# Staging the padded projection weights in an exponentials' buffer, with the query part compacted later

## The chip, the cores and the metric

The kernel runs on one core of one Trainium2 chip. A core has a matrix engine (TensorE, PE in the profile; its weight loads are shown as PEld), a vector engine (VectorE, DVE), an engine for activations and scaled copies (ScalarE, ACT), a general engine (GpSimd, POOL) and a queue engine (SyncE, SP). Each runs its own instructions in order and waits for the others on semaphores. ScalarE, GpSimd and SyncE also issue DMA transfers. SBUF is the on-chip memory, PSUM the memory that TensorE writes to.

The metric is the device time of one execution in microseconds (us), as the median of several runs.

## The reference

Input x has 4 batches of 1024 tokens of 256 features. The function is one transformer block, each half with a norm before it and a norm of what it adds:

```
x = x + layernorm(attention(layernorm(x), Wqkv, Wout))
x = x + layernorm(ffn(layernorm(x), w1, w2, h1, h2, w3 and scales))

attention: q, k, v = x @ Wqkv.T in 16 heads of 16
           softmax(q k^T / 4) v, then @ Wout.T
ffn:       h = silu(x w1^T s1) * (x w2^T s2)
           h = gelu(h h1^T t1);  h = gelu(h h2^T t2);  h w3^T s3
```

The weights of the feed-forward part hold only -1, 0 and 1. All is float32.

## The kernel before, in words

The attention goes over 4 batches, in each over 4 groups of 4 heads (`HPG`), in each over two halves of 512 queries, and in each over 8 chunks of 128 keys. For a chunk and two heads a score tile `s` of 128 x 1024 is made by two matmuls (line 471), ScalarE writes its exponentials `e` (line 472), and four matmuls add `e` times the values into `acc` (line 479). The exponentials lie in a ring of four buffers, `ring` (line 227), each for two score tiles. The first ring buffer is also zeroed at the start (`zeros`, line 228), and matmuls of these zeros into the tile `idle` (line 979) keep TensorE at work while the first input arrives. The feed-forward part follows after all four batches.

Scores are exact to about float32 though they are made with a shorter format: the projections are split into a rounded part (`hi`, line 330, by ScalarE) and the rest (`lo`, line 331, by VectorE). DMAs copy rows of both into stacked operands `sk` and `sq` (lines 410 to 423, issued in line 419), so that one matmul sums the products of the parts. For the first batch there are 64 such copies: 16 for each of k and q in each of the two halves of the tokens. Their issue is dealt out over three engines in turn (line 975): in every 8 copies ScalarE issues one, GpSimd four and SyncE three.

What comes before the first score tile, for batch 0, is the prologue, in this order. SyncE issues the load of the first half of x, the key part of the projection weights `wqk`, the second half of x, and the query part of `wqk` (lines 153 and 189 to 193). `wqk` is padded in memory: each head has 32 columns (`SLOT`), of which 16 (`DH`) hold weights. It lands in a staging tile, `slotted`, and ScalarE copies the 16 columns of each head into the dense tile `wqk_sb` (line 191), first the key part (`w` = 1), then the query part (`w` = 0). The staging tile is in a pool of its own, `load`, at the right side of SBUF, which is closed after these copies. The pool `work` is opened at the right side after it (line 239).

VectorE takes the mean and variance of x's rows (lines 96 and 97), GpSimd the root (`rstd`, line 106), and VectorE writes the normalised rows into `xn`, a tile of the pool `work` (line 297, recorded at line 114). TensorE transposes `xn` into `pt` (line 307), ScalarE copies that to `xT` (line 308, recorded at line 268), and TensorE projects: k first, then q (`project`, lines 322 to 333; the matmuls are recorded at line 265, their output is `p`). After each projection the stack copies are issued. All that is done for the first half of the tokens and then for the second. Then come the first values `v[0]` (`pv`, copied to `cv`), and the score tiles begin. GpSimd places the values into `vaug` (line 449), which `acc` needs.

All of it is emitted in the order of the program (`manual_schedule`, line 152): each engine executes what it is given in the order in which the code calls it. The loop that orders the prologue is in lines 983 to 992. In the attention's main loop, side work (projections of further batches, values, endings) is put between the tiles by a planner, `Side`, which counts slots and does not look at the hardware; the change does not touch it.

Of the kernel before, what the change touches and what calls it, by code (L numbers as in the profile page):

```python
# [9 lines left out]
F32 = mybir.dt.float32  # L10
# [8 lines left out]
P = 128  # L19
HEADS = 16  # L20
DH = 16
SLOT = 32
# [4 lines left out]
RING = 8  # L27
# [10 lines left out]
NQ = 512  # L38
# [4 lines left out]
@with_exitstack  # L43
def tile_attention_ffn_block(ctx: ExitStack, tc: tile.TileContext, x, wqk, wv, wo, w1, w1s, w2, w2s, h1, h1s, h2, h2s, w3, w3s, out):

    nc = tc.nc
    B, S, D = x.shape
    bad = ctx.enter_context(tc.tile_pool(name="flag", bufs=1)).tile([1, 1], I32, name="bad")
    tile_fast(tc, x, wqk, wv, wo, w1, w1s, w2, w2s, h1, h1s, h2, h2s, w3, w3s, out, bad)
    failed = nc.values_load(bad[0:1, 0:1], min_val=0, max_val=1 << 24)
    with tc.If(failed > 0):
        tile_general(tc, x, wqk, wv, wo, w1, w1s, w2, w2s, h1, h1s, h2, h2s, w3, w3s, out)  # L70
# [47 lines left out]
def tile_fast(ctx: ExitStack, tc: tile.TileContext, x, wqk, wv, wo, w1, w1s, w2, w2s, h1, h1s, h2, h2s, w3, w3s, out, bad):  # L118
    nc = tc.nc
    B, S, D = x.shape  # L120
    HID = w1.shape[1]
    DC = D // P
# [17 lines left out]
    def pieces(h, view):  # L140

        t, n = NH + (TPQ - 1) * h, TPQ * h
        return (slice(n, n + 1), view[:, h : h + 1, :]), (slice(n + 1, n + TPQ), view[:, t : t + TPQ - 1, :])

    def load_x(b, halves=range(NH)):
        view = x[b].rearrange("(t p) d -> p t d", p=P)
        for h in halves:
            for at, tokens in pieces(h, view):
                nc.sync.dma_start(out=xs[b][:, at, :], in_=tokens)
# [31 lines left out]
    with ExitStack() as actx, ExitStack() as rctx:  # L181
        aw = actx.enter_context(tc.tile_pool(name="aw", bufs=1, side="right"))

        wqk_sb = aw.tile([P, DC, 2, HEADS, DH], F32, name="wqk_sb")
        wv_sb = aw.tile([P, DC, D], F32, name="wv_sb")
        wo_sb = aw.tile([P, DC, D], F32, name="wo_sb")
        with tc.tile_pool(name="load", bufs=1, side="right") as load:
            slotted = load.tile([P, DC, 2, HEADS, SLOT], F32, name="slotted")
            for w in (1, 0):
                nc.sync.dma_start(out=slotted[:, :, w], in_=wqk.rearrange("(c p) (k h s) -> p c k h s", p=P, k=2, s=SLOT)[:, :, w])  # L190
                nc.scalar.copy(wqk_sb[:, :, w], slotted[:, :, w, :, 0:DH])
                if w:
                    load_x(0, [1])
        nc.scalar.dma_start(out=wv_sb, in_=wv.rearrange("(c p) d -> p c d", p=P))

        def load_rest():
# [23 lines left out]
        for i in range(2):  # L220
# [1 line left out]
            nc.gpsimd.memset(t, 0.0)  # L222
            nc.gpsimd.memset(t[:, :, :, DH : DH + 1], 1.0)
            vaug.append(t)

        rp = rctx.enter_context(tc.tile_pool(name="ring", bufs=1))
        ring = [rp.tile([P, 2, 2, NQ], F32, name=f"e{i}") for i in range(RING // 2)]
        zeros = ring[0][:, 0, 0]
        nc.vector.memset(zeros, 0.0)

        on = [aw.tile([P, TPQ, D], F32, name=f"on{h}") for h in range(NH)]

# [177 lines left out]
        def copies(g, w, c0=0, c1=S):  # L410

            m, i = g // GPT, g % 2

            def copy(u, j, n):
                def run(queue):
                    k = "hi" if (j // 2 == 0 if w == 0 else j % 2 == 0) else "lo"
                    r = (g % GPT) * HPG * DH + (2 * u + n) * DH
                    o = n * ROWS + j * DH
                    queue.dma_start(out=stacks[w, i, u][o : o + DH, c0:c1].bitcast(F32), in_=cq[w, m, k][r : r + DH, c0:c1].bitcast(F32))

                return run

            return [copy(u, j, n) for u in range(2) for j in range(PARTS) for n in range(2)]
# [33 lines left out]
        stacked, slotted, outstanding = [None] * 2, [None] * 2, []  # L457
# [201 lines left out]
        side = Side()  # L659
# [323 lines left out]
        for h in range(NH):  # L983
            for step in xt[h][TPQ // 2 :]:
                step.run()
            for w, step in zip((1, 0), qk[0][h]):
                step.run()
                for i, copy in enumerate(copies(0, w, h * NQ, (h + 1) * NQ)):
                    copy(queues[i % len(queues)])
                if w and h + 1 < NH:  # L990
                    for step in normalise[h + 1]:
                        step.run()
# [18 lines left out]
        while weighed < len(tiles):  # L1011
            n = end = made
# [3 lines left out]
            if made == len(tiles):  # L1016
                n = made
# [4 lines left out]
            if n - weighed >= 4 and made - weighed + TURN - 2 <= RING and tiles[weighed][3] != NT - 2 and side.next_is_heavy():  # L1022
                n = weighed + 2
            while weighed + 2 <= n:
                b, g, h, c, _ = tiles[weighed]
# [258 lines left out]
```

## Time and profile before

| what | value |
|---|---|
| time before, median of 3 runs | 1292.86 us (1292.04 to 1293.14) |
| span of the profiled execution | 1291.6 us |
| its own time outside that span | not given apart; the median of the runs is 1.26 us above the span |
| TensorE busy | 1244.4 us, 96% of the span |
| VectorE busy | 729.1 us, 56% |
| ScalarE busy | 699.2 us, 54% |
| GpSimd busy | 120.2 us, 9% |
| DMA traffic | 107.03 MB, mean 83 GB/s |
| first start of `acc` (line 479) | 34.34 us after the span's start |

The page of the profile describes one execution. It gives each engine's busy time, the span cut into 40 slices with the busy share in tenths, and the chain of work that ended last. Other answers of the trace list who waited for whom, the instructions in order of time (start, length, engine, line, operation, tile written and tiles read, and in brackets the idle time before it and what ended that), and for chosen stretches the busy time of each engine with the clock that TensorE was granted as a share of full speed.

### The profile page before, as it was taken

What the parts mean: (1) busy time and instruction counts of PE and PEld (TensorE: products, weight loads), DVE (VectorE), ACT (ScalarE), POOL (GpSimd) and SP (SyncE); (2) the same over time, 40 slices, a digit from 0 to 9 for tenths busy, and PEclk for the clock granted to TensorE, in tenths of its full rate; (3) what the DMA queues carried; (4) which work ended last, traced back from release to release, by engine and by line L of the source; (5) the groups of instructions that cost most, each with busy time, mean ns of one, the idle gap of its engine ahead of it and who ended that gap; (6) DMA issues with size and microseconds to landing.
All of it is one profiled execution on the core that took longest, in us unless ns stands there. A gap on an engine that the chain in (4) does not pass through costs nothing.

```text
span 1291.6 us, 21098 instructions
## 1 busy us (share of the span) xinstructions
PE 1244.4 (96%) x8104; PEld 770.0 (60%) x8104; DVE 729.1 (56%) x1625; ACT 699.2 (54%) x855; POOL 120.2 (9%) x166
## 2 busy tenths in 40 slices
PE   7999999999999999998999999999999999999995
PEld 3333334333333334333788888888888888888885
DVE  3466557765677556755643725637456374463533
ACT  3788788888889888998421413214132141331410
POOL 6211012111121110000000000000000000000000
PEclk8999899999999999999999999999999999999998
DMA  4676644665574654462320000201102011020000
GB/s 130 159 188 161 146 121 119 145 162 122 117 178 117 154 117 100 99 163 85 134 92 1 25 1 1 74 17 41 49 1 66 25 42 49 1 66 9 17 1 20
DMA packets 65679, 107.03 MB, mean 83 GB/s; under 512 B 12960, under 2 KB 39200, under 8 KB 65568
## 3 DMA queue, kind: packets, MB, share of 16 engines
q1 hardware_dynamic: 57680, 80.93, 25.4%
q0 software_dynamic: 7360, 24.12, 6.0%
q8 instruction: 66, 1.08, 0.4%
q10 hardware_dynamic: 528, 0.52, 0.2%
q14 instruction: 45, 0.37, 0.1%
HBM read 48.38 MB, written 23.59 MB: 56 GB/s over the span
## 4 chain that ended last, share of the span: by engine, by line
PE 76%; DVE 10%; ACT 8%; issue 2%; DMA 2%; SPq 1%; ACTq 0%; POOL 0%; POOLq 0%; DVEq 0%
PE ph L814 36%; PE acc L479 13%; PE s L471 8%; ACT e L472 6%; PE pz L867 4%; PE p L265 4%; PE pg L814 3%; PE py L265 2%; PE pv L265 2%; DVE sg L830 2%; DVE top L488 2%; DVE ha_lo L819 1%; DVE st L96 1%; PE po L518 1%; ACT sg L828 1%
## 5 line engine op out<-in xcount | busy, mean ns | idle before, releaser
L472 ACT ACTIVATE e<-s 128x1024 f32<-128x1024 f32 x512 | 482.6, 1035 | 59.4 <-PE s L471 49.7
L479 PE MATMUL acc<-e,vaug 128*32 128x512 f32 x2048 | 256.8, 604 | 1.4 <-POOL vaug L449 1.3
L850 ACT ACTIVATE a<-ph,h_scale 128x512 f32<-128x512 f32 x128 | 81.0, 685 | 301.4 <-PE ph L814 301.4
L471 PE MATMUL s<-sq,sk 64*128 64x512 f32 x1024 | 186.0, 443 | 18.2 <-ACT e L472 13.4
L814 PE MATMUL ph<-hb_hi,h 128*128 128x512 f32 x512 | 199.5, 390 | 0.0
L814 PE MATMUL ph<-hb_lo,h 128*128 128x512 f32 x512 | 199.4, 389 | 0.0
L471 PEld LDWEIGHTS s<-sq,sk 64*128 64x128 f32 x1024 | 86.1, 185 | 139.0 <-ACT e L472 114.6
L488 DVE TENSOR_TENSOR top<-top,e 128x512 f32<-128x512 f32 x192 | 134.8, 702 | 16.0 <-ACT e L472 10.8
L106 POOL TENSOR_TENSOR rstd<-ve,minus_half 128x4 f32<-128x4 f32 (+1 forms) x33 | 38.3, 1162 | 834.9 <-DVE ve L104 834.9
L479 PEld LDWEIGHTS acc<-e,vaug 128*32 128x32 f32 x2048 | 49.3, 109 | 107.1 <-issue 102.8
L814 PEld LDWEIGHTS ph<-hb_lo,h 128*128 128x128 f32 x512 | 96.1, 188 | 20.1
L814 PEld LDWEIGHTS ph<-hb_hi,h 128*128 128x128 f32 x512 | 96.1, 188 | 20.2
L851 DVE CAST ha_hi<-a 128x512 fp32r<-128x512 f32 x64 | 27.1, 423 | 142.7 <-ACT a L850 142.7
L814 PE MATMUL ph<-ha_hi,sq 128*128 128x512 f32 x256 | 101.8, 398 | 0.4
L814 PE MATMUL ph<-ha_lo,sq 128*128 128x512 f32 x256 | 99.8, 390 | 0.0
L814 PE MATMUL ph<-ha_lo,sk 128*128 128x512 f32 x256 | 99.7, 390 | 0.0
L814 PE MATMUL ph<-ha_hi,sk 128*128 128x512 f32 x256 | 99.7, 389 | 0.0
L828 ACT ACTIVATE sg<-pg,w_scale 128x512 f32<-128x512 f32 x64 | 43.3, 688 | 56.0 <-DVE ha_lo L819 45.6
L830 DVE SCALAR_TENSOR_TENSOR sg<-pg,w_scale,sg 128x512 f32<-128x512 f32 x64 | 47.1, 745 | 46.3 <-ACT sg L828 46.1
L851 DVE CAST hb_hi<-a 128x512 fp32r<-128x512 f32 x64 | 27.0, 422 | 71.5 <-ACT a L850 71.5
L265 PE MATMUL p<-xT,wqk_sb 128*32 128x512 f32 x512 | 62.3, 608 | 2.9 <-DVE on L496 1.7
L814 PEld LDWEIGHTS ph<-ha_hi,sq 128*128 128x128 f32 x256 | 48.1, 188 | 13.1 <-DVE sg L830 3.4
(165 smaller groups left out, 1640.7 us busy)
## 6 DMA issues: line engine op xcount, KB each, us to landing
w<-in_h_dram POOLq DMA_DIRECT2D x16, 512.0 KB, 5.6
h_r<-wr POOLq DMA_DIRECT2D x16, 512.0 KB, 3.8
x<-in_h_dram SPq DMA_DIRECT2D x32, 256.0 KB, 2.7
top_d<-top SPq DMA_DIRECT2D x30, 256.0 KB, 2.3
folded<-top_d SPq DMA_DIRECT2D x30, 256.0 KB, 3.3
sk<-ck1hi SPq DMA_DIRECT2D x64, 64.0 KB, 2.7
sk<-ck1lo SPq DMA_DIRECT2D x64, 64.0 KB, 2.9
sq<-cq1hi SPq DMA_DIRECT2D x64, 64.0 KB, 2.6
```

Of the source, the lines that this page charges most:

```text
L106: nc.gpsimd.tensor_tensor(rstd[:, :n], ve[:, :n], self.minus_half[:, :n], ALU.pow)
L265: nc.tensor.matmul(o[j : j + SLOT, :], w[:, j : j + SLOT], i, **flags)
L471: nc.tensor.matmul(s[:, a, :], stacks[1, g % 2, u][r, c * P : (c + 1) * P], stacks[0, g % 2, u][r, h * NQ : (h + 1) * NQ], start=True, sto ...
L472: nc.scalar.activation(pair(k)[:, u], s, AF.Exp)
L479: nc.tensor.matmul(acc[SLOT * i : SLOT * (i + 1), :], vaug[g % 2][:, c, i, :], pair(k)[:, i // 2, i % 2, :], start=c == 0, stop=c == NT - 1)
L488: nc.vector.tensor_max(top, top if c > 1 else pair(k - 2)[:, :, :, 0:P], pair(k)[:, :, :, 0:P])
L814: nc.tensor.matmul(p, homes[n][c][:, m * P : (m + 1) * P], half[:, c, :], start=c == 0 and k == 0, stop=c == len(homes[n]) - 1 and k == 1)
L828: nc.scalar.activation(sg, p[:, 0, :], AF.Silu, scale=scales["w1"][:, m : m + 1])
L830: nc.vector.scalar_tensor_tensor(sg, p[:, 1, :], scales["w2"][:, m : m + 1], sg, ALU.mult, ALU.mult)
L850: nc.scalar.activation(a, p[:, j, :], AF.Gelu, scale=scales[n][:, m : m + 1])
L851: nc.vector.tensor_copy(o[0][:, m, :], a)
L867: nc.tensor.matmul(p[t], half[:, c, t * P : (t + 1) * P], homes["w3"][c], start=c == 0 and k == 0, stop=c == HC - 1 and k == 1)
```

## The change

The staging tile and its pool are taken away. The ring of exponentials' buffers is allocated earlier, at the place where the staging pool was, with the zeroing of its first buffer. The padded weights are loaded into the last ring buffer, seen with the shape of the staging tile, by the same two DMAs in the same order. The two copies into `wqk_sb` become calls of `compact`: the one for the key part follows directly after the loads' issue; the one for the query part is called in the prologue's loop, for the first half of the tokens, between k's stack copies and q's projection. In ScalarE's order it so comes behind the copies of the first transposed x, k's rounded part and the two stack copies that ScalarE issues for k; the load of the values' weights, `wv`, is issued before it and no longer after it.

```diff
@@ -184,13 +184,20 @@
-        with tc.tile_pool(name="load", bufs=1, side="right") as load:
-            slotted = load.tile([P, DC, 2, HEADS, SLOT], F32, name="slotted")
-            for w in (1, 0):
-                nc.sync.dma_start(out=slotted[:, :, w], in_=wqk.rearrange("(c p) (k h s) -> p c k h s", p=P, k=2, s=SLOT)[:, :, w])
-                nc.scalar.copy(wqk_sb[:, :, w], slotted[:, :, w, :, 0:DH])
-                if w:
-                    load_x(0, [1])
+        rp = rctx.enter_context(tc.tile_pool(name="ring", bufs=1))
+        ring = [rp.tile([P, 2, 2, NQ], F32, name=f"e{i}") for i in range(RING // 2)]
+        zeros = ring[0][:, 0, 0]
+        nc.vector.memset(zeros, 0.0)
+        padded = ring[-1].rearrange("p a b n -> p (a b n)").rearrange("p (c k h s) -> p c k h s", c=DC, k=2, s=SLOT)
+
+        def compact(w):
+            nc.scalar.copy(wqk_sb[:, :, w], padded[:, :, w, :, 0:DH])
+
+        for w in (1, 0):
+            nc.sync.dma_start(out=padded[:, :, w], in_=wqk.rearrange("(c p) (k h s) -> p c k h s", p=P, k=2, s=SLOT)[:, :, w])
+            if w:
+                load_x(0, [1])
+        compact(1)
         nc.scalar.dma_start(out=wv_sb, in_=wv.rearrange("(c p) d -> p c d", p=P))
@@ -222,11 +229,6 @@
-
-        rp = rctx.enter_context(tc.tile_pool(name="ring", bufs=1))
-        ring = [rp.tile([P, 2, 2, NQ], F32, name=f"e{i}") for i in range(RING // 2)]
-        zeros = ring[0][:, 0, 0]
-        nc.vector.memset(zeros, 0.0)
@@ -984,6 +986,8 @@
             for w, step in zip((1, 0), qk[0][h]):
+                if (h, w) == (0, 0):
+                    compact(0)
                 step.run()
                 for i, copy in enumerate(copies(0, w, h * NQ, (h + 1) * NQ)):
```

## The prediction

> **What bounds the kernel now.** First the page: TensorE is busy 96% of the span and makes up 76% of the chain, so time is lost only where it waits. In its 40 slices the first alone shows 7.
>
> ```profile
> PE 1244.4 (96%) x8104; PEld 770.0 (60%) x8104; DVE 729.1 (56%) x1625; ACT 699.2 (54%) x855; POOL 120.2 (9%) x166
> ...
> PE   7999999999999999998999999999999999999995
> ```
>
> So I read the first 40 us: waits, then the chain, then the timeline. The waits (who for whom, total, times, longest) show VectorE held 3.9 us by ScalarE's copy of the weights, and TensorE by VectorE behind it:
>
> ```profile
> DVE xn L114 <- ACT wqk_sb L191: 3.9, 1, 3.9
> PE pt L307 <- DVE xn L114: 3.1, 1, 3.1
> ```
>
> Normalising reads no weights. The code explains the wait: `xn` is in a pool opened where the staging tile's pool was closed, on the same side, so it takes that memory over. The timeline shows when `xn` could have started: its last real input, `rstd`, ends at 6.38+1.03=7.41; it starts at 10.15.
>
> ```profile
> 6.38 1.03 POOL L106 TENSOR_TENSOR rstd<-ve,minus_half 128x4 f32<-128x4 f32 x1 [2.89 <-DVE ve L104]
> 9.44 0.62 ACT L191 COPY wqk_sb<-slotted 128x512 f32<-128x512 f32 x1 [2.67 <-DMA slotted<-in_wqk_dram]
> 10.15 1.38 DVE L114 TENSOR_SCALAR xn<-x,mv,rstd 128x256 f32<-128x256 f32 x4 [3.86 <-ACT wqk_sb L191]
> ```
>
> The chain (start, length, what) runs through that copy and k's projection, then through the issue of stack copies, whose last query copy releases the scores at 28.81:
>
> ```profile
> 3.17 6.25 DMA slotted<-in_wqk_dram
> 9.44 0.62 ACT wqk_sb L191
> ...
> 12.92 3.62 PE p L265 x16
> 16.56 0.61 ACT ck0hi L268
> ...
> 25.80 2.81 DMA sq<-cq0lo
> ...
> 33.89 0.40 POOL vaug L449
> 34.29 0.04 issue
> 34.34 1.06 PE acc L479 x8
> ```
>
> I measure all by the start of `acc` at 34.34: after it the engines release each other in a fixed order, and I pass a shift there 1:1 to the end.
>
> Last the windows cut at the clock's steps (PE busy, then, after the other engines, the granted clock). Full clock is lost after 1.38 and 1.93 us of work in 3.41 us, and kept after 2.00 (101.73):
>
> ```profile
> 6.16:9.57 3.41, 1.38 (x4) 0.31 (x2) 0.14 (x1) 0.74 (x2) 1.03 (x1) 1.00 0.69 252
> 9.57:12.98 3.41, 2.36 (x12) 1.61 (x16) 2.73 (x10) 1.12 (x3) 0.00 (x0) 0.50 0.30 77
> 12.98:16.40 3.41, 3.41 (x20) 0.79 (x22) 0.82 (x4) 0.57 (x1) 1.01 (x1) 0.50 0.00 0
> 26.64:30.05 3.41, 1.93 (x14) 1.13 (x18) 0.00 (x0) 2.13 (x3) 3.41 (x8) 1.00 0.61 138
> 30.05:33.46 3.41, 3.41 (x34) 1.59 (x24) 0.41 (x1) 1.43 (x2) 3.04 (x7) 0.50 0.57 119
> 101.73:105.14 3.41, 2.00 (x21) 0.89 (x15) 2.32 (x5) 1.37 (x2) 0.00 (x0) 1.00 0.19 58
> ```
>
> [...] steps at 9.57, 16.40, 30.05 and 33.46 lie on a grid of 3.41; four matmuls of k's projection take 0.85 us before 16.40 and 0.43 after. That the grid's phase differs between executions one profile can't show. [...] 2.30 us of transposes in 9.57 to 12.98 didn't raise the clock. [...]
>
> **The change part by part.** *Removed: the wait of `xn`.* It starts 0.05 after `rstd`, at 7.45: 2.70 earlier. The rest of the first half's chain, to k's rounded copy `ck0hi`, took 16.56-10.15=6.41 at half clock.
>
> *Clock.* The warming matmuls end at 7.53. Today the array idles until 10.62 and falls to half at 9.57. With transposes from 7.9 the window to 9.57 holds 1.38+1.65=3.0 us of work, so I expect full clock to stay. k's 16 records then take 4x0.43=1.71 for 3.41, the transposes before some 0.25 less: `ck0hi` starts at 7.45+6.41-1.95=11.9, which is 4.65 earlier.
>
> *Moved: the query copy, 0.62 us.* It comes after k's projection in program order, so on ScalarE behind `ck0hi` (0.60) and two DMA issues (17.18 to 18.42, 1.24). From `ck0hi`'s start: 0.60+0.03+1.24+0.04=1.91, copy 0.62, 0.07 to release: q's projection starts 2.60 later, where today it follows k's at once. At 1.71+0.24, `cq0hi` starts at 11.9+4.55=16.5; today at 16.56+1.91. So q is 2.64 later relative to k. Who waits? POOL and SP are issuing k's copies till 5.1 and 5.4 after `ck0hi` started (21.67 and 21.96 today); q's rounded part, 4.55+0.60+0.28=5.4, is 0.3 late for POOL, nothing for SP. Without that cover it would be 2.64.
>
> *What is late next.* TensorE takes q, then the second half's transposes: `cq0hi` to transposed x 1.85 (18.47 to 20.31), 0.65 to k, 1.99 to its `ck0hi`: 16.5+4.49=20.9, end 21.5, first POOL copy 21.8. POOL has been free since 21.0 and issues 16 copies at 0.476 until 29.4, against 33.09 today: 3.7 earlier. TensorE meanwhile ends the second half (8x0.43 from 19.8, no waits), the first values (1.73, done 25.1) and three score tiles to 25.8; the second values take 1.73 to 27.7 for 3.33 today, as the gap between 26.3 and 28.8 that cost the clock is gone. Their copy (0.74+0.14) is done before POOL, so `vaug` starts at 29.5 and `acc` at 29.95: **4.4 earlier in this grid**.
>
> *Other phases.* Today's half-clock stretch at 30.05 is chance. In a grid where the gap at 26.3 to 28.8 loses no window, the second values end 1.6 earlier and `vaug` waits for POOL's 33.09 instead: `acc` at 33.6, 0.7 earlier. I give that half the grids: -0.35. After the change, the array idles from 11.8 to 14.5; a window whose end falls between 13.9 and 16.2 goes to half within q, costing 1.7 where it ends ahead of 14.5 and the rest of q's time after it: (0.6x1.7+1.7x0.85)/3.41, -0.72 on average. k at half in a tenth of the grids: 0.1x1.95, -0.2. Sum 4.4-0.35-0.72-0.2=**3.1 us**.
>
> *Costs of nothing.* Weights land in the last ring buffer: same bytes, same two issues at the same places of SP's queue; its first exponential is tile 6, after 37 us, on the engine that read it. The zeroing of the first ring buffer keeps its place on VectorE. The `wv` load (256 KB, 1 issue) goes out at 6.8, no longer 9.45, into traffic of some 400 GB/s: others land up to 0.7 later. x's second half (8.13) is read from 8.9 to 10, the query weights (9.42) at 13.8; uncovered it would cost 0.7. The key copy stays at 6.16.
>
> Sum against the profiled execution: span 1291.6-3.1=1288.5. The median is 1292.86, 1.26 above that span (what lies around it, and spread); kept as it is: **1289.8 us**.
>
> **Rivals.** *A, likeliest: as above,* 2 to 4.6 us faster, 1288.2 to 1290.9.
>
> *B: k stays at half clock[...].* For it: 1.38 us of matmuls lost the clock[...]. Against: the window at 101.73 kept it with 2.00, of which 0.76 transposes. Then `ck0hi` starts near 13.4 to 13.9, q at 16.0 to 16.5, partly at half, `cq0hi` near 19.3, the second half's `ck0hi` at 23.8, POOL done at 32.3, `acc` at 32.8 to 33.5: 0.9 to 1.5 faster, 1291.7, inside the noise.
>
> *C, slower: the gap before q breaks the clock for the whole second half.* From `cq0hi` 20.15 (k and q at half), second k starts 22.65; the second projections, both pairs of values take 6.9 at full and 13.7 at half. At full `acc` comes at 32.8; all at half, 39.6: 5.3 late, 1298.1. It decides (2.6 late) from 4.1 of the 6.9 on. Against it: 12.98 to 16.40 shows that one full window restores the clock.
>
> *D: the wait stays,* because `xn` or the transposes hang on something else that lands at 9.4; then q's 2.64 less POOL's cover of 2.4 leaves 1293.1. The listed waits of `xn` name only the weights and `rstd`, so hardly.
>
> **How the numbers follow.** Below 0.2%, 2.6 us, a measurement of this kernel tells nothing from no change. A 0.68, of which 0.50 above 2.6 us; B 0.18, D 0.04, C 0.10 with other losses. Faster 0.50; same 0.18+0.18+0.04=0.40; slower 0.10. Unknown are the clock's phases (each half-clock window later, like 142.69 to 149.52, is worth up to 1.7), so the range goes beyond A: low 1287.0 (4.4 and one such window saved, near 6), high 1293.8 (B and D plus half a window); A's own is 1288.2 to 1290.9.
>
> **What would show it.** Right: `xn` at 7.4 to 7.6, k's 16 records within 2.0 us, the query copy at 13.8 behind two DMA issues with 2.7 us of idle TensorE around it, POOL's last stack copy near 29.4, `acc` near 30, `vaug` waiting on POOL rather than the values' copy. Wrong: granted clock 0.5 between 9.6 and 13, second values again at half, or a later stretch at half clock that eats the 4 us.

## The result and the profile after

The changed kernel takes 1288.69 us (median, 1287.05 to 1291.96), the kernel before beside it 1293.14: ratio 0.9969, 95% interval 0.9956 to 0.9981. Measured again later, beside other runs of before, it took 1290.17 against 1293.01: ratio 0.9982, 0.9974 to 0.9991. In microseconds the two intervals are 2.5 to 5.7 and 1.2 to 3.4 faster. Single runs of either kernel spread over some 5 us and more. The mean of all 28 runs of the changed kernel is 1290.1, of before 1293.1 to 1293.2 in each of the later sets: 3.0 us or 0.23% faster. The forecast was 1289.8, 3.1 faster, which lies inside both intervals.

The wait of `xn` is gone. In the timeline of the changed kernel it follows `rstd` at once (7.35), k's rounded part `ck0hi` starts at 11.79 and no longer at 16.56, and the copy of the query weights stands at 13.70, behind two issues of DMAs on ScalarE's queue (ACTq). Its weights had landed long before: in the kernel below that keeps both copies at the head, the same copy ran at 9.53.

```profile
6.28 1.03 POOL L106 TENSOR_TENSOR rstd<-ve,minus_half 128x4 f32<-128x4 f32 x1 [2.79 <-DVE ve L104]
7.35 1.38 DVE L114 TENSOR_SCALAR xn<-x,mv,rstd 128x256 f32<-128x256 f32 x4 [1.15 <-POOL rstd L106]
...
9.80 1.92 PE L267 MATMUL p<-xT,wqk_sb 128*32 128x512 f32 x16 [0.25 <-ACT xT L270]
...
11.79 0.60 ACT L270 ACTIVATE ck0hi<-p 128x512 fp32r<-128x512 f32 x1 [1.55 <-PE p L267]
12.42 1.24 ACTq L421 DMA_DIRECT2D sk<-ck0hi  x2
...
13.70 0.62 ACT L194 COPY wqk_sb<-e 128x512 f32<-128x512 f32 x1 [1.31 <-issue]
```

k's 16 records take 1.92 us to the last end, at full clock. In the chain, which counts to the next engine's start, they take 1.97, where the half-clock ones of before took 3.62. In place of the wait stands a new one, named in the list of waits for the first 40 us:

```profile
PE p L267 <- ACT wqk_sb L194: 2.6, 1, 2.6
```

In the windows cut at the steps of this execution's clock (PE busy, then, last but two, the granted clock) that gap leaves 0.77 us of work between 11.67 and 15.09; q, from 14.37 on, mostly ran at half:

```profile
8.26:11.67 3.41, 3.16 (x23) 1.10 (x23) 2.63 (x11) 1.09 (x2) 0.53 (x1) 1.00 0.25 86
11.67:15.09 3.41, 0.77 (x12) 0.29 (x12) 2.02 (x5) 1.22 (x2) 2.85 (x6) 1.00 0.22 48
15.09:18.50 3.41, 3.41 (x18) 1.43 (x11) 0.46 (x1) 0.60 (x1) 2.03 (x5) 0.50 0.52 106
18.50:21.91 3.41, 2.21 (x23) 0.77 (x25) 0.23 (x1) 1.09 (x2) 3.41 (x8) 1.00 0.51 106
```

At the end of the prologue, by the timeline, the values' copy is done at 29.32+0.69=30.01, but `vaug` starts when GpSimd has issued its last stack copies, at 30.90. `acc` starts at 31.36, before it was 34.34: 2.98 earlier.

```profile
29.32 0.69 DVE L273 TENSOR_SCALAR cv<-pv 128x512 f32<-128x512 f32 x1 [3.72 <-PE pv L267]
...
29.94 0.96 POOL L421 DMA_DIRECT2D sq<-cq0lo  x2
30.90 0.41 POOL L451 COPY vaug<-cv 128x256 f32<-128x256 f32 x1
...
31.36 0.64 PE L481 MATMUL acc<-e,vaug 128*32 128x512 f32 x4 [1.21 <-POOL vaug L451]
```

This lead is handed on unchanged at first: at tiles 10 to 60 of the exponentials it is 2.96 to 2.98. The two profiled spans differ by more, 1291.6-1285.4=6.2. Most of the rest is a stretch at half clock that the profiled execution of before has from 142.69 to 149.52, and the changed one has not. The same two stretches of before and then of after:

```profile
139.00:142.70 3.70, 1.26 (x11) 0.72 (x7) 3.46 (x11) 2.50 (x3) 0.00 (x0) 1.00 0.51 84
142.70:149.50 6.80, 6.25 (x26) 2.14 (x26) 1.38 (x2) 1.94 (x2) 0.00 (x0) 0.50 0.63 146
```

```profile
139.00:142.70 3.70, 3.46 (x28) 1.45 (x28) 0.94 (x2) 1.94 (x2) 0.00 (x0) 1.00 0.48 117
142.70:149.50 6.80, 6.80 (x77) 2.80 (x76) 3.35 (x10) 5.55 (x6) 1.17 (x2) 1.00 0.67 148
```

Between tiles 97 and 99 of the exponentials the lead grows from 4.55 to 6.89 us. Other profiles of faster kernels below do have this stretch, and the second profile of the changed kernel has half of it (139.62 to 143.03), so it is no part of the change's worth: the spans of one profile each show twice the gain.

### The profile page after: what moved, and what is told of

The parts are those of the page before. It is cut to its first block, busy times and chain, and to the rows that moved or that the text cites. A ratio compares the mean times of both kernels' runs of the same rounds, so it can differ in the third digit from the quotient of the medians.

```text
span 1285.4 us, 21095 instructions
## 1 busy us (share of the span) xinstructions
PE 1237.9 (96%) x8104; PEld 767.9 (60%) x8104; DVE 728.2 (57%) x1625; ACT 699.9 (54%) x855; POOL 121.3 (9%) x166
## 4 chain that ended last, share of the span: by engine, by line
PE 75%; DVE 8%; ACT 8%; DMA 3%; issue 3%; SPq 1%; ACTq 1%; POOL 0%; POOLq 0%; DVEq 0%
PE ph L816 36%; PE acc L481 12%; PE s L473 8%; ACT e L474 6%; PE pz L869 4%; PE pg L816 4%; PE p L267 4%; PE py L267 2%; DVE sg L832 2%; PE pv L267 2%; DVE top L490 1%; DVE ha_lo L821 1%; DVE st L96 1%; PE po L520 1%; SPq L421 1%
```

## The experiments

Theory W: the wait of `xn` is what costs, and the late query copy gives some of the gain back through q and the clock. Rivals: that the moved copy carries the gain (M), that memory placement does, or that only later half-clock stretches differ (L). The first four kernels ran beside the same runs of before (median 1293.35), the next four beside others (1293.01), the last two beside a third set (1293.17).

**The staging tile alone moved.** Both copies stay together at the head.

```diff
         compact(1)
+        compact(0)
         nc.scalar.dma_start(out=wv_sb, ...)
...
-                if (h, w) == (0, 0):
-                    compact(0)
```

> Only the staging tile is moved into the last ring buffer; both copies of the weights stay together, ahead of the first transposed x on ScalarE. Theory W (the gain is the wait of xn that goes; the late query copy gives some of it back): xn at 7.4, the first transposed x waits for the query copy and comes at 10.1 instead of 9.15, k's rounded part at 12.7 instead of 11.8, but q follows k at once and POOL never stands still: its stack copies end near 29.3, acc starts at 29.5 to 30.3, the time is 3 to 5 us below that before, within 1.2 us of the changed kernel. Rival M (it is the moved copy that frees the prologue): less than 1.5 us below before, acc not before 32.5. Rival L (the gain lies in later half-clock stretches, by chance): acc anywhere, and timed runs spread over before's.

Measured: 1289.5 us, ratio 0.9973 (0.9965 to 0.9982). In its profile `xn` starts at 8.34 (x's statistics came a microsecond later in this execution), the last stack copy is issued by 30.16, and `acc` follows:

```profile
8.34 1.38 DVE L114 TENSOR_SCALAR xn<-x,mv,rstd 128x256 f32<-128x256 f32 x4 [1.15 <-POOL rstd L106]
...
12.79 0.60 ACT L271 ACTIVATE ck0hi<-p 128x512 fp32r<-128x512 f32 x1 [1.55 <-PE p L268]
...
30.61 1.47 PE L482 MATMUL acc<-e,vaug 128*32 128x512 f32 x8 [2.22 <-POOL vaug L452]
```

W holds on the time: the memory alone gives the whole gain. M falls. POOL ended 0.9 later than expected: its 32 issues took 16.5 us from first to last, where before they took 15.6.

**The query copy ahead of k's projection.**

```diff
+            if h == 0:
+                compact(0)
             for w, step in zip((1, 0), qk[0][h]):
-                if (h, w) == (0, 0):
-                    compact(0)
                 step.run()
```

> The query copy is called between the first half's transposed x and k's projection, so that it stands ahead of k's rounded part on ScalarE. Theory W: it runs at 10.2 to 10.9 while TensorE projects k, and costs nothing; q follows k at 11.5, its rounded part comes at 13.7 instead of 17.4, TensorE has no gap, POOL issues its 32 copies without a stop and ends near 28.3; acc starts at 28.7 to 29.4 instead of 31.4. Time 0.7 to 2 us below the changed kernel, 4.5 to 6 below before. Rival (POOL and SP hide where q stands): the same as the changed kernel within 0.4 us.

Measured: 1289.94 us, ratio 0.9973 (0.9963 to 0.9982): not better than the changed kernel. The timeline shows that the copy hid as meant, between the transposed x and `ck0hi`, and q followed k without a gap (one run of 32 records):

```profile
10.58 3.64 PE L267 MATMUL p<-xT,wqk_sb 128*32 128x512 f32 x32 [0.25 <-ACT xT L270]
10.90 0.62 ACT L194 COPY wqk_sb<-e 128x512 f32<-128x512 f32 x1
...
14.48 0.60 ACT L270 ACTIVATE cq0hi<-p 128x512 fp32r<-128x512 f32 x1 [1.31 <-PE p L267]
```

But TensorE now reaches the score tiles before their operands have landed, as it did before the change (there they waited 1.8 us in all for `sq`, up to 28.81). The gap ahead of q became a gap ahead of the scores, and the clock fell in the window after it:

```profile
21.90:25.31 3.41, 1.30 (x13) 0.48 (x3) 0.58 (x1) 1.46 (x2) 2.98 (x7) 1.00 0.58 132
25.31:28.72 3.41, 3.41 (x25) 1.59 (x29) 0.00 (x0) 2.10 (x3) 3.41 (x8) 0.50 0.56 117
```

Also, GpSimd's issue took 16.5 us from first to last in place of the 15.6 of before, with one wait of 0.8 us for an earlier copy to land. `acc` started at 30.91; in this profile `vaug` waited 0.5 us for the values' copy, whose matmuls ran partly at half clock, and not for POOL. The expectation of another 0.7 to 2 us failed, so with four warming matmuls the late query copy is not seen to give anything back. The rival, that SP and POOL hide where q stands, held on the time; how much of the earlier q the lost clock and the slower issue each took was not separated.

**The gap filled with matmuls of zeros.**

```diff
                     compact(0)
+                    for _ in range(WARM - 1):
+                        nc.tensor.matmul(idle, zeros[:, 0:P], zeros, start=True, stop=True)
                 step.run()
```

> The changed kernel with three matmuls of zeros (2.56 us at full clock) between k's and q's projection. Theory W (the gap loses the clock in two thirds of the grids, 0.7 us on average): granted clock stays 1.0 from 6 to 26 us, q takes 1.7 to 1.8 us, acc starts at 29.8 to 30.3, the time is 0.4 to 1 us below the changed kernel, and its runs spread less. Rival (the clock in the gap is nothing): same time as the changed kernel within 0.3 us.

Measured: 1289.77 us, ratio 0.9975 (0.9964 to 0.9986). The clock stayed full from 7.66 to 137.37 and `acc` started at 30.51, but the time is that of the changed kernel. In this profile's prologue the mechanism is there (`acc` 18.3 us after k's rounded part started; 19.6 where q ran at half); on the average of runs it is worth too little to be seen with intervals of this width.

**One warming matmul in place of four.** This and the three later kernels without warming leave out three of the four matmuls of zeros at the start, whose product nobody reads.

```diff
-        for _ in range(WARM):
+        for _ in range(1):
             nc.tensor.matmul(idle, zeros[:, 0:P], zeros, start=True, stop=True)
```

> The changed kernel with one warming matmul in place of four at the start. Theory W (full clock through k is worth some 1.95 us at k's rounded part and more behind it): k's 16 records take 3.4 us, k's rounded part starts at 13.6 to 13.9, q falls to half or is at half, acc starts at 32.5 to 34, the time is 1.5 to 3.5 us above the changed kernel. Rival (transposes and the short k don't feel the clock): within 0.5 us of the changed kernel.

Measured: 1292.99 us, ratio 1.0000 (0.9992 to 1.0008). No gain is left, although `xn` starts at 7.56. k's rounded part came at 12.78, a microsecond earlier than expected, since the clock rose to full at 11.37 within k (behind that step 12 of its records took 1.33 us). Then the late query copy held q until 15.36, and q ran at half (0.50 granted from 14.78 to 18.19):

```profile
12.78 0.60 ACT L270 ACTIVATE ck0hi<-p 128x512 fp32r<-128x512 f32 x1 [1.82 <-PE p L267]
...
14.68 0.62 ACT L194 COPY wqk_sb<-e 128x512 f32<-128x512 f32 x1 [1.31 <-issue]
...
15.36 3.30 PE L267 MATMUL p<-xT,wqk_sb 128*32 128x512 f32 x16 [2.65 <-ACT wqk_sb L194]
```

The second half's k came at 25.09 (22.14 in the changed kernel, 22.95 before) and `acc` at 34.32.

**The wait put back.** The kernel with the staging tile alone moved, and one more VectorE copy of a column that nobody reads.

```diff
-        for step in norm[0] + normalise[0] + norm[1]:
+        for step in norm[0]:
+            step.run()
+        held = small.tile([P, 1], F32, tag="held", name="held", bufs=1)
+        nc.vector.tensor_copy(held, wqk_sb[:, 0, 0, 0, 0:1])
+        for step in normalise[0] + norm[1]:
             step.run()
```

> The kernel with only the staging tile moved (both weight copies together at the head), and ahead of the normalising a VectorE copy of one column of the query weights, which nobody reads: the wait is back, the memory stays as in the changed kernel. Theory W (the wait is what costs): xn at 10.1 to 10.4, array idle from 7 on, granted clock 0.5 through k's projection, k's rounded part near 16.6, acc at 33.6 to 34.8, time within 1 us of before, 1293.2. Rival (placement in memory, or what else the new layout changes): time within 1 us of 1289.7.

Measured: 1293.09 us, ratio 1.0003 (0.9995 to 1.0011). Up to k's rounded part the profile is that of before, step by step:

```profile
10.07 0.15 DVE L987 COPY held<-wqk_sb 128x1 f32<-128x1 f32 x1 [3.48 <-ACT wqk_sb L194]
10.14 1.38 DVE L114 TENSOR_SCALAR xn<-x,mv,rstd 128x256 f32<-128x256 f32 x4
...
16.54 0.60 ACT L271 ACTIVATE ck0hi<-p 128x512 fp32r<-128x512 f32 x1 [3.00 <-PE p L268]
...
33.72 1.06 PE L482 MATMUL acc<-e,vaug 128*32 128x512 f32 x8 [1.68 <-POOL vaug L452]
```

`acc` comes 0.6 earlier than in the profile of before, since here the second values ran at full clock (1.93 us; 3.33 before) and `vaug` waited for POOL, whose last issue ended at 33.26.

Same memory, same loads, the wait alone: the whole gain is lost. Placement falls as a rival, and so does L as the cause of the gain in the means.

**The kernel before with one warming matmul in place of four** (the edit as above).

> The kernel before with one warming matmul in place of four. Theory W (before, the clock that the warming raised is lost in the wait, ahead of k): the same time as before within 0.5 us, acc at 33.6 to 34.8. Rival (warming is worth about 3 us by itself, whatever xn waits for, as the changed kernel without it suggests): 2 to 3.5 us above before.

Measured: 1292.21 us, ratio 0.9996 (0.9987 to 1.0006), `acc` at 33.55. Before the change the warming bought nothing that can be measured.

**The first values placed by VectorE.**

```diff
-                nc.gpsimd.tensor_copy(
+                (nc.gpsimd if t1 == NT else nc.vector).tensor_copy(
                     vaug[g % 2][:, t0:t1, :, 0:DH], ...
```

> The changed kernel with the first placing of values into vaug done by VectorE and not by GpSimd, where it stands behind 32 issues of stack copies. Theory W (POOL's issue is what is late next): vaug starts within 0.2 us of the end of the values' copy, at 28.6 to 30.1 instead of 29.5 to 30.9, acc 0.5 to 0.9 us earlier than in the changed kernel at the same granted clock; time 0.4 to 1 us below it. Rival (something else holds acc): same time within 0.3 us.

Measured: 1289.76 us, ratio 0.9978 (0.9968 to 0.9988), 0.4 below the changed kernel of the same set, with intervals that overlap almost wholly. The prologue did what was expected: `vaug` at 30.24, 0.1 after the values' copy, while GpSimd issued stack copies until 31.11.

```profile
29.44 0.69 DVE L273 TENSOR_SCALAR cv<-pv 128x512 f32<-128x512 f32 x1 [3.83 <-PE pv L267]
...
30.07 1.04 POOL L421 DMA_DIRECT2D sq<-cq0lo  x2
30.24 0.29 DVE L451 COPY vaug<-cv 128x256 f32<-128x256 f32 x1
```

So POOL does hold `vaug` in the changed kernel. Whether 0.9 us at that place is kept to the end stays open. The two profiles of that set can't decide it: q lost its clock in this one (half from 16.28 on) and kept it in that of the changed kernel, so `acc` starts at 30.68 and 30.66, and by tile 10 they still stand equal (39.37 and 39.35).

**The changed kernel once more.**

> The changed kernel once more, for more of its runs and a second profile beside the others. Theory W: k's rounded part at 11.7 to 12.4; where the windows of the clock miss the gap before q, acc at 29.9 to 30.2, where they hit it, to 31.5; mean time 3 to 4 us below before. Rival L (the gain lies in later half-clock stretches): at equal stretches at half clock after 100 us no gain remains.

Measured: 1290.17 us, ratio 0.9982 (0.9974 to 0.9991); mean 2.8 below before. In this profile k's rounded part started at 12.41 and `acc` at 30.66. Its clock stayed full through the gap, with less work in two windows than I had held enough (1.75 and 1.89 us; the window behind them, 20.15 to 23.57, was at 1.00 too):

```profile
12.41 0.60 ACT L270 ACTIVATE ck0hi<-p 128x512 fp32r<-128x512 f32 x1 [1.56 <-PE p L267]
...
30.66 1.06 PE L481 MATMUL acc<-e,vaug 128*32 128x512 f32 x8 [1.61 <-POOL vaug L451]
```

```profile
13.33:16.74 3.41, 1.75 (x16) 0.42 (x16) 1.74 (x5) 0.62 (x1) 3.39 (x7) 1.00 0.37 85
16.74:20.15 3.41, 1.89 (x20) 1.14 (x20) 0.69 (x1) 1.68 (x3) 3.08 (x7) 1.00 0.61 130
```

**The other places of the query copy, without warming.** With both copies at the head, and with the copy ahead of k (the edits as above).

> Only the staging tile moved (both weight copies at the head), with one warming matmul in place of four. Theory P (without the clock the late query copy is what eats the gain: the array idles 2.6 us ahead of q, which keeps q and the second half at half clock): q follows k at once here, k's rounded part at 14.0 to 14.6, POOL's copies end at 31 to 32, acc at 31.7 to 33; time 1 to 2.5 us below before and below the changed kernel without warming (mean 1292.8). Rival K (without the clock the end of the wait is worth nothing wherever the copy is): within 0.7 us of before.

> The query copy between the first transposed x and k's projection, with one warming matmul in place of four. Theory P: as with both copies at the head, but x is transposed 0.9 us earlier: k's rounded part at 13.2 to 13.9, acc at 31 to 32.5, time 1.5 to 3 us below before. Rival K: within 0.7 us of before.

Measured: 1291.04 us, ratio 0.9982 (0.9973 to 0.9991), and 1290.94, ratio 0.9982 (0.9973 to 0.9992). In their profiles, in that order, `acc` started at 32.36 and 31.94. With one warming matmul these two kernels are 2.3 us below before by their ratios, and the changed kernel, with its late query copy, is not. So K falls, and with one warming matmul the place of the copy matters; with four, no difference is seen. Two comparisons are not clear of noise. Against the kernel before that also has one warming matmul, these two gain 1.1 us by the means and 1.8 by the ratios, and the intervals overlap. And in these two places the three further warming matmuls gain 0.0009, about as much as each ratio is uncertain. The ratios to before together (each known to about 0.001 either way):

| where the query copy stands | four warming matmuls | one |
|---|---|---|
| before (wait of `xn`) | 1 | 0.9996 |
| changed kernel: behind k's rounded part | 0.9969 and 0.9982 | 1.0000 |
| both copies at the head | 0.9973 | 0.9982 |
| ahead of k's projection | 0.9973 | 0.9982 |

None of the kernels tried is measurably faster than the changed one. In their profiles `acc` starts at 33.55 to 34.34 in the four with ratios from 0.9996 to 1.0003, at 31.94 and 32.36 in the two with one warming matmul and 0.9982, and at 30.51 to 31.36 in all others. So the starts of `acc` fall into the same three groups as the times.

## Why the prediction was right

- *The wait goes, `xn` at 7.45:* 7.35 and 7.97 in two profiles, right behind `rstd` in both. Put back alone, it cost all of the gain. Right.
- *k at full clock, `ck0hi` at 11.9:* 11.79. Right, and in the changed kernel the gain hangs on it: with one warming matmul it gained nothing. It is no need everywhere: with both copies at the head and one warming matmul k ran at half (`ck0hi` at 14.29, after ScalarE had waited 3.12 us for k; 3.01 before, 1.55 in the changed kernel), and 0.9982 was left.
- *The query copy at 13.8, 2.6 us of idle array, cover by POOL and SP:* copy at 13.70, gap 2.65. Right on the time: kernels in which q follows k at once are no faster. POOL waited 0.3 us for q's rounded part where q kept its clock, as predicted, and 1.4 where it lost it.
- *POOL late next, `vaug` waiting on it:* shown by the timeline and by the kernel in which VectorE places the values. Predicted POOL end 17.5 us after `ck0hi` started; in the profile with a full clock it was 30.20-12.41=17.8.
- *`acc` at 29.95, 4.4 earlier, in a grid that leaves q its clock:* such a profile had 30.66, with `ck0hi` itself 0.5 later than predicted: 18.25 us between the two, 18.05 predicted. Where q lost its clock, 31.36. That is 0.7 later than the sum took for such a grid, 0.5 of it because x's statistics came later in that execution.
- *Before in another grid, `acc` at 33.6 behind POOL:* the kernel with the wait put back shows it, at 33.72 behind POOL's 33.26. Right.
- *The chances of the clock, -0.35-0.72-0.2:* the weakest terms, my estimate from the windows of one profile, which took it that the grid of clock steps can lie elsewhere in another execution. It can: the step at 15.09 in the changed kernel is 15.09-9.57=5.52 us behind the one at 9.57 before, 1.6 windows of 3.41. How often each position comes isn't shown. I took 1.93 us of work in a window for too little, and two windows with 1.75 and 1.89 kept the clock, which would make the share smaller than two thirds. In the three profiles that have this gap unfilled behind four warming matmuls q lost the clock in two, too few to tell; filling the gap brought nothing measurable. The runs of before and after spread by 5 us and more. That the sum is 3.1 and the difference of the means 3.0 is in part luck, as the two sets gave 4.0 and 2.3 by their ratios; it doesn't confirm these parts one by one.
- *Rival B, half clock through k,* came true with the warming removed: I had priced it at 0.9 to 1.5 us faster; measured, with k only in part at half, it was 0.0 (0.0008 either way, 1 us), so the low end of the price is just inside the noise. In the profile `acc` came at 34.32, priced at 32.8 to 33.5, as q and the second half's k lost more of the clock than I allowed (0.50 granted from 14.78 to 18.19 and from 21.61 to 25.02). A window of mainly transposes did keep the clock: with both copies at the head (14.08 to 17.49) one with 2.29 us of work, 1.64 of it transposes. C and D didn't come.

## What to carry to other kernels

Look at what a wait is really for: normalising waited for weights it doesn't read, because a released staging tile lent it its memory. A buffer that is idle at that time can take the weights instead: here the last exponentials' buffer, whose first exponential is written at 34.62 in the changed kernel. Before pricing the gap that a moved copy opens, ask what else ends last there: with four warming matmuls the issue of DMAs covered it, with one it ate the whole gain. And look at what follows a warming: before the change the clock that it had raised at 6.16 (its weight loads came 0.85 us apart up to 6.01, the last 0.50 later) fell again at 9.57, after 1.38 us of work in between, ahead of the first transpose at 10.62.

## What I had not expected

Three of the four warming matmuls are worth nothing measurable before the change (0.9996 without them, 0.9987 to 1.0006) and, within the noise, all of the gain in the changed kernel. Where q follows k at once they are worth at most a part (0.9973 with them, 0.9982 without). Removing a gap in TensorE's order moved it to the next place where operands were late, with the same loss of clock there (1.30 us of work between 21.90 and 25.31, then 0.50). And equal work did not always keep the clock. In the profile of before, a window with 1.93 us, 1.62 of it score matmuls, lost it at 30.05; one with 1.93 us of projections (0.98) and `acc` (0.95) kept it at 245.09. In the second profile of the changed kernel 1.75 us of mainly projections kept it.

Over all twelve profiles, cut into such windows from the first recorded step of the clock to 1270 us, the busy time alone doesn't decide: the clock stayed full after as little as 1.75 us and fell after as much as 2.23, of which 1.49 were score matmuls (one of the kernels with one warming matmul):

```profile
540.52:543.93 3.41, 2.23 (x16) 0.73 (x16) 3.28 (x7) 3.41 (x5) 0.00 (x0) 1.00 0.35 63
543.93:547.34 3.41, 3.41 (x20) 1.10 (x13) 0.69 (x1) 1.81 (x2) 0.00 (x0) 0.50 0.00 0
```

What decides beside the busy time isn't shown. In these profiles every window ahead of a fall held some work, 0.77 us at the least (the changed kernel, 11.67 to 15.09).
